# Two-layer transformer on one core: copies of the turned rows shared between ScalarE and VectorE, and four smaller moves in layer 1's attention

## The chip, the cores and the metric

The kernel runs on 1 core of one Trainium2 chip. The metric is the device time of the whole program in microseconds; the median of the timed runs is compared before and after. A core has a matrix engine (TensorE, PE), three engines for elementwise work (VectorE, DVE; ScalarE, ACT; GpSimd, POOL) and queues that start transfers (SyncE, SP, and GpSimd's own for gathers). Each engine works through its own instructions in order, and waits on semaphores for the others. TensorE writes to PSUM, which has eight banks here, each with room for 128 x 512 float32.

## The reference

Two layers, each attention and then a feed-forward part, with a layer norm (no scale) after each residual, on x of 8 x 512 x 512 float32. Layer 0 has causal attention with 16 heads and eight experts of which each token takes two. Layer 1, cut to what matters here:

```python
# attention: 8 heads of 64, keys and values shared by 4 heads each
nrm = norm(x, axis=-1) * d ** -0.5
h = norm_scale * x / (nrm + 1e-8) * split_scale
q, k, v = h @ Wq.T, h @ Wk.T, h @ Wv.T
attn = softmax(q @ k.T / sqrt(64))
x = layernorm(x + (x + (attn @ v) @ Wo.T))
# feed-forward, weights as integers: W = (wq - 128) * scale
x = layernorm(x + (silu(x @ Wg.T) * (x @ Wu.T)) @ Wd.T)
```

## The kernel before

The rows are worked in 8 batches of 512 tokens; a batch has NT = 4 tiles of 128 rows and ND = 4 slices of 128 columns. The stages follow each other: attention of layer 0, routing and expert tiles, attention of layer 1 (`Attention1.batches`, about 1189 to 1772 us of the profile), and the integer feed-forward (`IntegerFfn`). The change lies in layer 1's attention.

**Preparing a batch** (`Attention1.prepare`): its rows are the experts' results. `fetch` gathers two rows for each token (GpSimd starts the transfers, L673). They are weighted and added to x, tile by tile, either by `add` on VectorE (two L680, then `stat`: L694 and L695) or, in the first batch of the stage, partly by `sum` on GpSimd (two pairs L689, L690 for a tile) with `stat` in a later step. `deviations` (GpSimd, L701 to L703) and `norm` (VectorE, L710, L711, four L714) make the normalised rows xn. `turn(c)` transposes column slice c of the four tiles by TensorE into one bank of PSUM (L1477) and copies it, scaled, to hT (L1478, ScalarE). `key`, `value` and `query` multiply hT with the weights (L1484, L1493, L1503), and ScalarE copies the results out.

**The batch itself** is run in eight steps of two units each, a unit being a pair of heads g and a tile of keys kt. In each step, TensorE first makes the scores of its two units (`score`, L1579), which ScalarE exponentiates (L1582); VectorE adds the exponentials of the step before to a total (`add`, L1590: one instruction in odd steps, two in even ones); then the step's other work is issued from the list `todo`; then TensorE multiplies the exponentials of the step before with the values (`product`, L1601). After the fourth tile of keys, `normalise` sums the total over the partitions by TensorE (L1609, to a bank "rs"), copies it by ScalarE (L931), inverts it (VectorE, L1612), scales the head pair's output (L1613), and GpSimd adds the inverse to a guard's total (L934).

**The list of other work** (`plan`): step 0 issues the gathers of batch b + 1, and queries go to steps 0, 1 and 3 (1, 3 and 5 in the first batch, 0, 1 and 5 in the last). From the second batch on, steps 2 to 5 `project` batch b - 1, a tile each (L1551; `residual`: L1557 and the statistics L1561, L1562; after the fourth tile GpSimd's L1565 and L1566 make rstd), and step 6 first normalises batch b - 1 on VectorE (`norm`, four L1572, which need rstd), then turns the four slices of batch b + 1 and projects its keys; step 7 makes its values and first query. In the last batch, steps 4 and 6 turn and split batch 0's rows for the feed-forward instead (`split`: L1022 on TensorE, L1023 on ScalarE, L1024 on VectorE). `weights.convert` (L994, L926) turns integer weights to floats in steps 1 and 7.

**What sets the order.** While this stage runs, `in_order` fixes the order of TensorE, VectorE, ScalarE and GpSimd to the one in which the code issues. Before it, among the expert tiles, only TensorE is so fixed, and after it, in the feed-forward, a scheduler places the instructions. PSUM: two banks, "mm", are shared by all of `self.mm` (turned slices, projections, "rs"); four hold scores, two hold the heads' outputs. Exponentials have four buffers.

**The first batch** is prepared piece by piece between expert tiles (`first_pieces`); the second is prepared inside the first, and so on.

**The end of the stage**: after the last step the remaining sums are made, then the last batch is projected with all four tiles' banks open: three of four head groups for each tile, `norm` of batch 6, then the fourth group of each tile, followed by `residual`. The feed-forward starts with L1055 (gate and up, 16 instructions each), L1058 on ScalarE, L1060 on VectorE, the split of the hidden values (L1063, L1064) and the down product L1069, whose weights come from L994.

Of the kernel before, what the change touches and what calls it, by code (L numbers as in the profile page):

```python
# [13 lines left out]
AF = mybir.ActivationFunctionType  # L14
ALU = mybir.AluOpType
# [3 lines left out]
P = 128  # L19
NB = 8  # L20
S = 512
D = 512
NT = S // P
ND = D // P
# [48 lines left out]
class Env:  # L73
# [19 lines left out]
    def open_stream(self, ctx, batches, **kw):  # L93

        resident = ctx.enter_context(self.tc.tile_pool(name=f"resident{batches[0]}", bufs=1, **kw))
        for b in batches:
            self.xs[b] = resident.tile([P, NT, D], F32, tag=f"x{b}", name=f"x_{b}")
# [904 lines left out]
class IntegerFfn:  # L1002
# [9 lines left out]
    def split(self, b, c, ps):  # L1012


        nc = self.nc
        if c == 0:
            pool = self.work if b % 2 else self.rows
            self.halves[b] = [pool.tile([P, ND, S], F32R, tag=f"rows{i}", name=f"x3_{part}")
                              for i, part in enumerate(("high", "low"))]
        high, low = self.halves[b]  # L1020
        for t in range(NT):
            nc.tensor.transpose(ps[:, ts(t, P)], self.env.xs[b][:, t, ts(c, P)], self.env.ident)  # L1022
        nc.scalar.copy(high[:, c, :], ps)  # L1023
        nc.vector.tensor_tensor(low[:, c, :], ps, high[:, c, :].bitcast(F32), ALU.subtract)  # L1024
# [420 lines left out]
class Attention1:  # L1445
# [17 lines left out]
    def prepare(self, b):  # L1463


        nc, own, w_qkv = self.nc, self.own, self.w_qkv
        st = self.state[b] = {"qT": [None] * ND}
        combine = Combine(self.router, b, self.rows, ("rows0", "rows1"))

        def norm():  # L1470
            st["xn"], st["scale"] = combine.norm()
            st["hT"] = own.tile([P, ND, S], F32, tag="hT", name="hT1")

        def turn(c):
            ps = self.mm([P, S], "ps_hT")
            for t in range(NT):
                nc.tensor.transpose(ps[:, ts(t, P)], st["xn"][:, t, ts(c, P)], self.env.ident)  # L1477
            nc.scalar.activation(st["hT"][:, c, :], ps, AF.Copy, scale=self.nss[:, c : c + 1])  # L1478

        def key():  # L1480
            hT = st["hT"]
            ps = self.mm([P, S], "ps_k1")
            for c in range(ND):
                nc.tensor.matmul(ps, lhsT=w_qkv[:, 4, ts(c, P)], rhs=hT[:, c, :], start=c == 0, stop=c == ND - 1)  # L1484
            st["kT"] = own.tile([P, S], F32, tag="kT", name="kT", bufs=2)
            nc.scalar.copy(st["kT"], ps)

        def value():
            hT = st["hT"]
            ps = self.mm([P, NT, P], "ps_v1")  # L1490
            for t in range(NT):
                for c in range(ND):
                    nc.tensor.matmul(ps[:, t, :], lhsT=hT[:, c, ts(t, P)], rhs=w_qkv[:, 5, ts(c, P)],  # L1493
                                     start=c == 0, stop=c == ND - 1)
            st["v"] = own.tile([P, NT, P], F32, tag="v", name="v1", bufs=2)
            nc.scalar.copy(st["v"], ps)

        def query(g):

            hT = st["hT"]  # L1500
            ps = self.mm([P, S], "ps_q1")
            for c in range(ND):
                nc.tensor.matmul(ps, lhsT=w_qkv[:, c, ts(g, P)], rhs=hT[:, c, :], start=c == 0, stop=c == ND - 1)  # L1503
            st["qT"][g] = (self.work if g % 2 else own).tile([P, S], F32, tag="qT", name="qT")
            nc.scalar.copy(st["qT"][g], ps)  # L1505

        return {"fetch": combine.fetch, "add": combine.add, "sum": combine.sum, "stat": combine.stat, "deviations": combine.deviations, "norm": norm,
                "turn": turn, "key": key, "value": value, "query": query}

    def first_pieces(self):  # L1510
# [15 lines left out]
    def batches(self, work, p_sc, p_av, weights, split):  # L1526
        env, nc, guard, state, HD = self.env, self.nc, self.guard, self.state, self.HD
        xs = env.xs
        scale = 1.0 / math.sqrt(HD)
# [14 lines left out]
        def project(b, t):  # L1544
            ps = self.mm([P, D], "ps_o1")
            project_groups(b, t, ps, range(ND))
            residual(b, t, ps)

        def project_groups(b, t, ps, groups):
            for c in groups:  # L1550
                nc.tensor.matmul(ps, lhsT=state[b]["aoT"][:, c, ts(t, P)], rhs=w_out[:, c, :],  # L1551
                                 start=c == 0, stop=c == ND - 1)

        def residual(b, t, ps):
            st = state[b]
            x = xs[b][:, t, :]
            nc.vector.scalar_tensor_tensor(x, x, st["scale"][t], ps, ALU.mult, ALU.add)  # L1557
            if t == 0:
                st["stats"] = small.tile([P, NT, 6], F32, name="stats1")
                st["mv"] = small.tile([P, NT, 2], F32, name="mv1")  # L1560
            nc.vector.bn_stats(out=st["stats"][:, t, :], in_=x)  # L1561
            nc.vector.bn_aggr(out=st["mv"][:, t, :], in_=st["stats"][:, t, :])  # L1562
            if t == NT - 1:
                st["rstd"] = rstd = small.tile([P, NT], F32, name="rstd1")
                nc.gpsimd.tensor_scalar(rstd, st["mv"][:, :, 1], LN_EPS, None, ALU.add)  # L1565
                nc.gpsimd.tensor_tensor(rstd, rstd, env.neg_half, ALU.pow)  # L1566

        def norm(b):
            st = state.pop(b)
            for t in range(NT):  # L1570
                x = xs[b][:, t, :]
                nc.vector.tensor_scalar(x, x, st["mv"][:, t, 0:1], st["rstd"][:, t : t + 1], ALU.subtract, ALU.mult)  # L1572
# [43 lines left out]
        def plan(b):  # L1616


            todo = [[] for _ in range(ND * NT // 2)]
            here = pieces.pop(b)  # L1620
            first, final = b == 0, b == NB - 1
            then = None if final else self.prepare(b + 1)
            if not final:
                pieces[b + 1] = then
                todo[0] += [lambda t=t: then["fetch"](t) for t in range(NT)]
            for g, i in zip((1, 2, 3), (1, 3, 5) if first else (0, 1, 5) if final else (0, 1, 3)):
                todo[i].append(lambda g=g: here["query"](g))
            if b:
                for t, i in enumerate((2, 3, 4, 7) if final else (2, 3, 4, 5)):
                    todo[i].append(lambda t=t: project(b - 1, t))  # L1630
                if not final:
                    todo[6].append(lambda: norm(b - 1))
            if final:
                for c, i in enumerate((4, 6, 6, 6)):
                    todo[i].append(lambda c=c: split(0, c, self.mm([P, S], "ps_xT")))
            else:
                if first:

                    for t, i in ((1, 1), (2, 2), (3, 3)):
                        todo[i].append(lambda t=t: then["sum"](t))  # L1640
                        todo[i + 1].append(lambda t=t: then["stat"](t))
                for t, i in ((0, 2),) if first else ((0, 2), (1, 2), (2, 3), (3, 4)):
                    todo[i].append(lambda t=t: then["add"](t))
                todo[4].append(then["deviations"])

                todo[5].insert(0, then["norm"])
                todo[6] += [lambda c=c: then["turn"](c) for c in range(ND)]
                todo[6].append(then["key"])
                todo[7] += [then["value"], lambda: then["query"](0)]
            for i in (7,) if first else (1, 7):  # L1650
                todo[i] += [weights.convert, lambda: weights.load(work, 2, weights.FIRST)]
            return todo

        last = []
        for b in range(NB):
            for i, thunks in enumerate(plan(b)):
                units = [(b, u // NT, u % NT) for u in (2 * i, 2 * i + 1)]
                ps = [score(*unit) for unit in units]
# [4 lines left out]
                sums = [product(*unit) for unit in last]  # L1663
# [3 lines left out]
        for unit in last:  # L1667
            add(*unit)
        sums = [product(*unit) for unit in last]
        sums[-1]()  # L1670

        b = NB - 1
        banks = [self.mm([P, D], "ps_o1") for _ in range(2)]
        banks += [p_sc.tile([P, 2, S], F32, tag="sc", name="ps_o1")[:, 0, :] for _ in range(2)]
        for t in range(NT):
            project_groups(b, t, banks[t], range(ND - 1))
        norm(b - 1)
        for t in range(NT):
            project_groups(b, t, banks[t], (ND - 1,))
            residual(b, t, banks[t])  # L1680
        return lambda: norm(b)


# [346 lines left out]
```

## Time and profile before

| | us |
|---|---|
| timed runs (3): median | 2297.6 |
| timed runs: lowest and highest | 2297.3, 2299.71 |
| the profiled execution: its own time | 2295.71 |
| the profiled execution: span from first to last instruction | 2293.9 |
| one batch of layer 1's attention (from one L1484 to the next, 1308.40 to 1381.47) | 73.1 |
| mean granted TensorE clock over the span | 0.994 |

The span is what the profile's times count from; the execution's own time has 1.8 us more around it. A line of the timeline gives the start, the time and the engine, then the program's line and the names of what is written and read; in square brackets stands how long the engine was idle before it and which engine's instruction ended that. "xN" says that N instructions were merged. PE stands for matmuls, PEld for loads of weights, which overlap them. A float32 matmul of 512 columns appears as two records.

### The profile page before, as it was taken

What the parts mean: (1) busy time and instruction counts of PE and PEld (TensorE: products, weight loads), DVE (VectorE), ACT (ScalarE), POOL (GpSimd) and SP (SyncE); (2) the same over time, 40 slices, a digit from 0 to 9 for tenths busy, and PEclk for the clock granted to TensorE, in tenths of its full rate; (3) what the DMA queues carried; (4) which work ended last, traced back from release to release, by engine and by line L of the source; (5) the groups of instructions that cost most, each with busy time, mean ns of one, the idle gap of its engine ahead of it and who ended that gap; (6) DMA issues with size and microseconds to landing.
All of it is one profiled execution on the core that took longest, in us unless ns stands there. A gap on an engine that the chain in (4) does not pass through costs nothing.

```text
span 2293.9 us, 24187 instructions
## 1 busy us (share of the span) xinstructions
PE 2240.5 (98%) x9430; PEld 1154.8 (50%) x9430; DVE 1245.0 (54%) x1974; ACT 648.2 (28%) x937; POOL 501.6 (22%) x493
## 2 busy tenths in 40 slices
PE   9999999999999999999998999999998999999997
PEld 3344444444444444444443334443343878888876
DVE  3457575666668432242216877777667544444443
ACT  2332323323324221111223323333332322222222
POOL 2231323413224231131125122321211000000000
PEclk9999999999999999999999999999999999999999
DMA  8010110101112234332233011100100100000000
GB/s 289 19 56 1 55 33 23 56 7 49 54 38 84 92 115 146 93 120 91 87 127 94 10 55 56 55 29 17 37 1 23 42 19 19 19 19 19 19 19 20
DMA packets 58444, 126.63 MB, mean 55 GB/s; under 512 B 6210, under 2 KB 6210, under 8 KB 58322
## 3 DMA queue, kind: packets, MB, share of 16 engines
q1 hardware_dynamic: 47040, 89.32, 11.1%
q0 software_dynamic: 10560, 34.61, 5.2%
q8 instruction: 77, 1.26, 0.2%
q10 hardware_dynamic: 722, 1.07, 0.1%
q14 instruction: 45, 0.37, 0.1%
HBM read 89.59 MB, written 35.39 MB: 54 GB/s over the span
## 4 chain that ended last, share of the span: by engine, by line
PE 76%; issue 8%; DVE 7%; DMA 4%; POOL 4%; ACT 2%; POOLq 0%; SPq 0%; ACTq 0%; DVEq 0%
PE ps_f L1069 7%; PE ps_g L1055 6%; PE ps_u L1055 6%; PE ps_gu L845 5%; PE ps_o L1216 5%; PE ps_o L1551 5%; PE av L1601 5%; PE sc L1579 4%; PE ps_q L1503 4%; PE ps_q L1200 4%; PE ps_k L1208 4%; PE ps_v L1193 4%; PE av L1288 3%; PE sc L1264 3%; PE ps_y L862 2%
## 5 line engine op out<-in xcount | busy, mean ns | idle before, releaser
L845 PE MATMUL ps_gu<-experts,xrT 128*128 128x512 f32 (+1 forms) x520 | 248.6, 601 | 0.0
L1268 ACT ACTIVATE p<-sc 128x2048 f32<-128x2048 f32 (+1 forms) x96 | 152.9, 1593 | 189.0 <-PE sc L1264 182.1
L1273 POOL TENSOR_SCALAR_AFFINE_SELECT p<-p 128x512 f32<-128x512 f32 x128 | 92.1, 734 | 380.1 <-ACT p L1268 376.6
L1060 DVE SCALAR_TENSOR_TENSOR hT<-ps_u,vec,sg 128x512 f32<-128x512 f32 x88 | 65.8, 748 | 201.4 <-PE ps_u L1055 201.4
L1069 PE MATMUL ps_f<-ffn_w,h_half 128*128 128x512 f32 x672 | 169.4, 392 | 1.1 <-DVE h_half L1064 1.1
L934 POOL TENSOR_TENSOR g_total<-g_total,r_inv 128x512 f32<-128x512 f32 x64 | 89.7, 1402 | 361.4 <-DVE r_inv L1612 286.2
L1612 DVE RECIPROCAL r_inv<-r_inv 128x512 f32<-128x512 f32 x32 | 106.8, 3339 | 105.4 <-ACT r_inv L931 105.4
L1582 ACT ACTIVATE p<-sc 128x1024 f32<-128x1024 f32 x128 | 124.1, 1021 | 130.3 <-PE sc L1579 119.7
L1296 DVE TENSOR_TENSOR p<-p 128x1536 f32<-128x1536 f32 (+2 forms) x96 | 129.3, 1346 | 38.5 <-POOL p L1273 21.5
L1055 PE MATMUL ps_g<-x_high,ffn_w 128*128 128x512 f32 x352 | 141.5, 402 | 3.0 <-DVE x L1557 3.0
L1069 PEld LDWEIGHTS ps_f<-ffn_w,h_half 128*128 128x128 f32 x672 | 124.5, 188 | 33.7 <-DVE h_half L1064 7.2
L848 DVE TENSOR_TENSOR h<-ps_gu,h 128x256 f32<-128x256 f32 x67 | 28.4, 424 | 205.2 <-ACT h L847 205.2
L1055 PE MATMUL ps_g<-x_low,ffn_w 128*128 128x512 f32 x352 | 139.4, 396 | 0.0
L1055 PE MATMUL ps_u<-x_high,ffn_w 128*128 128x512 f32 x352 | 139.2, 395 | 0.0
L1055 PE MATMUL ps_u<-x_low,ffn_w 128*128 128x512 f32 x352 | 139.2, 395 | 0.0
L1579 PE MATMUL sc<-qT,kT 64*128 64x512 f32 x512 | 127.9, 618 | 1.0 <-ACT qT L1505 0.7
L862 PE MATMUL ps_y<-experts,hT 128*128 128x512 f32 (+1 forms) x272 | 127.9, 592 | 0.5 <-ACT hT L856 0.5
L1200 PE MATMUL ps_q<-experts 128*128 128x512 f32 x256 | 120.4, 611 | 4.4 <-DMA experts<-in_xT 4.4
L845 PEld LDWEIGHTS ps_gu<-experts,xrT 128*128 128x128 f32 x520 | 89.6, 192 | 68.0 <-issue 68.0
L1601 PE MATMUL av<-p,v 128*64 128x512 f32 x512 | 123.8, 605 | 0.0
L1193 PE MATMUL ps_v<-experts 128*128 128x512 f32 x256 | 116.3, 602 | 2.4 <-DVE v L1195 2.4
L1208 PE MATMUL ps_k<-experts 128*128 128x512 f32 x256 | 117.5, 602 | 0.2 <-ACT r_inv L931 0.2
(256 smaller groups left out, 3544.5 us busy)
## 6 DMA issues: line engine op xcount, KB each, us to landing
results<-y SPq DMA_DIRECT2D x68, 256.0 KB
x<-in_x SPq DMA_DIRECT2D x8, 1024.0 KB
experts<-in_gate_up SPq DMA_DIRECT2D x8, 1024.0 KB
rows<-x SPq DMA_DIRECT2D x32, 256.0 KB
x<-rows SPq DMA_DIRECT2D x8, 1024.0 KB
experts<-in_xT SPq DMA_DIRECT2D x7, 1024.0 KB
out<-x SPq DMA_DIRECT2D x28, 256.0 KB
ffn_i<-in_wq_ffn SPq DMA_DIRECT2D x11, 512.0 KB
```

What stands on the lines that cost most here:

```text
L845: mm = nc.tensor.matmul(ps, lhsT=xT[:, c, :], rhs=self.weights(i, c), start=c == 0, stop=c == ND - 1)
L862: self.nc.tensor.matmul(ps, lhsT=hT[:, c, :], rhs=self.weights(i, ND + c), start=c == 0, stop=c == self.NI - 1)
L1055: nc.tensor.matmul(ps, lhsT=w[:, ts(dc, P)], rhs=x[:, dc, :], start=(dc, i) == (0, 0), stop=(dc, i) == (ND - 1, 1))
L1069: self.nc.tensor.matmul(os[t], lhsT=h[:, ts(t, P)], rhs=self.weights(2 * NHID + c), start=(c, i) == (0, 0), stop=(c, i) == (NHID - 1, 1))
L1193: nc.tensor.matmul(ps, lhsT=xts[b][:, c, ts(t, P)], rhs=wv[:, c, :], start=c == 0, stop=c == ND - 1)
L1200: nc.tensor.matmul(ps, lhsT=wq[:, g, ts(c, P)], rhs=xts[b][:, c, :], start=c == 0, stop=c == ND - 1)
L1208: nc.tensor.matmul(ps, lhsT=wk[:, g, ts(c, P)], rhs=xts[b][:, c, :], start=c == 0, stop=c == ND - 1)
L1268: nc.scalar.activation(p, sc[:, :, :width], AF.Exp, scale=scale)
L1296: nc.vector.tensor_tensor(total[:, :, P * kt :], total[:, :, P * kt :], p[:, :, at : at + w], ALU.add)
L1579: nc.tensor.matmul(sc[:, j, :], lhsT=st["kT"][hs, ts(kt, P)], rhs=st["qT"][g][hs, :], start=True, stop=True)
L1582: nc.scalar.activation(p, sc, AF.Exp, scale=scale)
L1601: nc.tensor.matmul(st["av"][HD * j : HD * (j + 1), :], lhsT=st["v"][:, kt, HD * j : HD * (j + 1)], rhs=p[:, j, :], start=kt == 0, stop=kt ...
```

## The change

Five edits, all in layer 1's attention.

1. `turn`: of the four copies of a batch's turned slices, those of c = 1 and 3 are made by VectorE (`tensor_scalar`), those of c = 0 and 2 stay with ScalarE. This holds for all eight batches, the first (among the expert tiles) too.
2. First batch: tiles 0 and 1 of the next batch are added on VectorE in steps 1 and 2, tiles 2 and 3 on GpSimd from steps 1 and 2, with their statistics two steps later. Before, tile 0 was added on VectorE in step 2, and tiles 1 to 3 on GpSimd from steps 1 to 3, with statistics one step later.
3. Last batch: the four splits of batch 0 go to steps 0, 2, 4 and 6, one each, instead of one in step 4 and three in step 6.
4. `residual` is cut into `residual` (L1557) and `statistics`. `project` still calls one after the other; at the end of the stage the four residuals come first and the four tiles' statistics after them.
5. At the end of the stage, the first bank is taken and the first three groups of tile 0 are issued ahead of the last sums (`sums[-1]()`); the second "mm" bank is taken after them.

```diff
-            nc.scalar.activation(st["hT"][:, c, :], ps, AF.Copy, scale=self.nss[:, c : c + 1])
+            if c % 2:
+                nc.vector.tensor_scalar(st["hT"][:, c, :], ps, self.nss[:, c : c + 1], None, ALU.mult)
+            else:
+                nc.scalar.activation(st["hT"][:, c, :], ps, AF.Copy, scale=self.nss[:, c : c + 1])
...
             residual(b, t, ps)
+            statistics(b, t)
...
             nc.vector.scalar_tensor_tensor(x, x, st["scale"][t], ps, ALU.mult, ALU.add)
+
+        def statistics(b, t):
+            st = state[b]
+            x = xs[b][:, t, :]
             if t == 0:
                 st["stats"] = small.tile([P, NT, 6], F32, name="stats1")
...
             if final:
-                for c, i in enumerate((4, 6, 6, 6)):
+                for c, i in enumerate((0, 2, 4, 6)):
                     todo[i].append(lambda c=c: split(0, c, self.mm([P, S], "ps_xT")))
             else:
                 if first:
 
-                    for t, i in ((1, 1), (2, 2), (3, 3)):
+                    for t, i in ((2, 1), (3, 2)):
                         todo[i].append(lambda t=t: then["sum"](t))
-                        todo[i + 1].append(lambda t=t: then["stat"](t))
-                for t, i in ((0, 2),) if first else ((0, 2), (1, 2), (2, 3), (3, 4)):
+                        todo[i + 2].append(lambda t=t: then["stat"](t))
+                for t, i in ((0, 1), (1, 2)) if first else ((0, 2), (1, 2), (2, 3), (3, 4)):
                     todo[i].append(lambda t=t: then["add"](t))
...
         sums = [product(*unit) for unit in last]
+
+        b = NB - 1
+        banks = [self.mm([P, D], "ps_o1")]
+        project_groups(b, 0, banks[0], range(ND - 1))
         sums[-1]()
-
-        b = NB - 1
-        banks = [self.mm([P, D], "ps_o1") for _ in range(2)]
+        banks.append(self.mm([P, D], "ps_o1"))
         banks += [p_sc.tile([P, 2, S], F32, tag="sc", name="ps_o1")[:, 0, :] for _ in range(2)]
-        for t in range(NT):
+        for t in range(1, NT):
             project_groups(b, t, banks[t], range(ND - 1))
         norm(b - 1)
         for t in range(NT):
             project_groups(b, t, banks[t], (ND - 1,))
             residual(b, t, banks[t])
+        for t in range(NT):
+            statistics(b, t)
         return lambda: norm(b)
```

## The prediction

> **What bounds the kernel now.** I read the busy times first, then the chain of waits, TensorE's waits in the changed stage (1188 to 1800 us), and the timeline around each.
>
> ```profile
> PE 2240.5 (98%) x9430; PEld 1154.8 (50%) x9430; DVE 1245.0 (54%) x1974; ACT 648.2 (28%) x937; POOL 501.6 (22%) x493
> ...
> PE 76%; issue 8%; DVE 7%; DMA 4%; POOL 4%; ACT 2%; POOLq 0%; SPq 0%; ACTq 0%; DVEq 0%
> ```
>
> TensorE (PE) is busy 98% of the span and leads the chain: an edit gains what it takes out of TensorE's gaps and loses what it adds to them. TensorE's waits in the stage:
>
> ```profile
> PE rs L1609 <- DVE total L1590: 6.5, 2, 4.9
> PE ps_hT L1477 <- ACT hT L1478: 3.6, 7, 0.8
> PE ps_g L1055 <- DVE x L1557: 3.0, 1, 3.0
> PE ps_xT L1022 <- DVE x_low L1024: 1.4, 1, 1.4
> PE ps_k L1484 <- ACT hT L1478: 1.4, 7, 0.2
> ```
>
> Columns: total us, times, longest. The change aims at these 15.9 us. Its largest edit, to the turnings, aims at 5.0 us in seven places; this is the second of them, in batch 1:
>
> ```profile
> 1305.09 1.40 PE L1477 MATMUL ps_hT<-ident,xn 128*128 128x128 f32 x8
> ...
> 1306.22 1.27 ACT L1478 ACTIVATE hT<-ps_hT,nss 128x512 f32<-128x512 f32 x2
> ...
> 1306.64 2.52 DVE L1590 TENSOR_TENSOR total<-total,p 128x1024 f32<-128x1024 f32 x2
> 1306.81 1.11 POOL L1565 TENSOR_SCALAR rstd<-mv 128x4 f32<-128x4 f32 x1 [5.03 <-DVE mv L1562]
> ...
> 1306.96 1.23 PE L1477 MATMUL ps_hT<-ident,xn 128*128 128x128 f32 x8 [0.47 <-ACT hT L1478]
> ...
> 1307.66 1.27 ACT L1478 ACTIVATE hT<-ps_hT,nss 128x512 f32<-128x512 f32 x2 [0.17 <-PE ps_hT L1477]
> 1308.00 2.05 POOL L1566 TENSOR_TENSOR rstd<-rstd,neg_half 128x4 f32<-128x4 f32 x1
> 1308.40 0.30 PEld L1484 LDWEIGHTS ps_k<-hT,attn_qkv 128*128 128x128 f32 x2 [0.44 <-ACT hT L1478]
> ...
> 1310.09 1.91 DVE L1572 TENSOR_SCALAR x<-x,mv,rstd 128x512 f32<-128x512 f32 x4 [0.93 <-POOL rstd L1566]
> ```
>
> Columns: start, duration, engine, line, instruction, idle time before it. Here ScalarE (ACT) is free and copies at once; VectorE (DVE) is working off L1590 and then waits for GpSimd's (POOL) L1566 before L1572.
>
> **Turnings, batches 1 to 6.** The copies of c = 1 and 3 go to VectorE, whose order in this stage is fixed by the program: the changed program issues them behind L1590 x2 and L1572 x4 (batch b-1's normalisation), none of which the change moves. That an instruction of VectorE doesn't overtake a waiting one, the first batch shows: L694 waited 9.26 us for GpSimd until 1205.88, and L680 behind it began only at 1206.70, though its rows had landed long before (they are the first two gathers, and GpSimd's L689 used the third at 1199.99). So the copy of c = 1 starts when L1572 ends, 1310.09 + 1.91 = 1312.00. No row has this copy on VectorE: nearest are L162, a plain copy from PSUM (681 ns), and L1202, a scaled one (750 ns). I take 0.75: done at 1312.75. From copy to TensorE the row shows 0.10 (c = 0's copy ends 1306.86, turning at 1306.96).
>
> In the changed program's waits the third and fourth turnings wait for ScalarE's copies alone; the key projection L1484 waits for VectorE's copy of c = 1. So TensorE turns c = 2 at 1306.96 as now, ScalarE copies it by about 1308.25, c = 3 is turned by 1308.9, and L1484 starts at 1312.85 instead of 1308.40: 4.45 us later, after 3.95 us of idle. The copy of c = 3 (to 1313.5) hides behind the first three quarters of L1484 (until 1312.85 + 3 x 0.86 = 1315.4); without that cover it would cost 0.75. Behind the two copies on VectorE stands L1612, whose sums TensorE delivers later still: nobody else waits. The other five batches show the same rows (0.47, 0.93 and 0.20 at 1380.0, 1383.2, 1381.5, and at 1672.4, 1675.5, 1673.8): 6 x 4.45 = 26.7 us. The saved wait of 0.67 is already taken off. If VectorE's work before the copy took the 0.68 copy or met no GpSimd contention in the normalisation, 0.1 each.
>
> **The clock behind these gaps.** Two gaps of TensorE in this stage are of that size, 4.87 and 3.00 us. Stretches of 5 us (busy times of PE, PEld, DVE, ACT, POOL; the granted clock; DMA):
>
> ```profile
> 1215.00:1220.00 5.00, 0.22 (x2) 0.00 (x0) 4.86 (x5) 1.94 (x2) 4.92 (x3) 1.00 0.00 0
> 1220.00:1225.00 5.00, 4.91 (x13) 1.63 (x14) 2.15 (x4) 1.84 (x4) 3.80 (x5) 0.66 0.01 3
> ...
> 1775.00:1780.00 5.00, 4.75 (x14) 3.75 (x15) 3.46 (x7) 1.72 (x2) 1.27 (x2) 0.66 0.51 197
> ```
>
> After each the clock is 0.66 over 5 us. L1609 to the next L1503 takes 4.50 us there (1220.09 to 1224.59) against 2.88 (1202.99 to 1205.87): 1.6 us. The 1.67 us gap before 1757.24 shows no such thing. A gap of 3.95 lies between the two that did; its place against the throttle's phase is unknown, so per gap 0 to 1.6. I take five of six: 8.0 us (bounds 0 and 9.6).
>
> [...]
>
> **Turnings elsewhere.** In batch 0 no L1572 stands in front: L1590 ends at 1234.15, the copy of c = 1 at 1234.9, the fourth turning (there it needs that bank) starts 0.45 later than 1234.46 and, without the present wait of 0.20, L1484 at 1235.5 instead of 1235.32: +0.2. Among the expert tiles two copies of 0.69 leave ScalarE for VectorE, which idles 3.82 us before its next L848: nothing; without that cover 2 x 0.75.
>
> **First batch's sums.** GpSimd loses two of six L689/L690 pairs, VectorE gets two L680 more (0.75 each) and stands no longer idle 9.26 us in L694:
>
> ```profile
> 1205.88 0.69 DVE L694 BATCH_NORM_STATS2 stats<-x 128x6 f32<-128x512 f32 x1 [9.26 <-POOL x L690]
> ...
> 1220.09 1.97 PE L1609 MATMUL rs<-total,ones 128*64 128x512 f32 x4 [4.87 <-DVE total L1590]
> ```
>
> The first two L680 now stand before the L1590 pair that the sums at 1202.99 need. Of those gathers, 83 packets of the gather queue's 640 had moved by 1197 and 240 by 1199, so, at 80 for each gather, the two land about 1197.4 and 1198.5, and at latest 1199.99. L680 ends 1199.25, L694/L695 0.87 later, L1590 x2 (2.56 alone, 3.4 beside GpSimd, the row at 1216.64) at about 1203.5: a wait of 0.5 (0 to 2). Then L680 x2 to 1205.6, statistics 1206.5, L1612/L1613 1210.5, L1590 1212.2, L694/L695 of t = 2 (GpSimd has its sum by about 1208) 1213.1, L1590 x2 1216.2, while the next sums are due at 1215.7: 0.5 (0 to 1). So 4.87 + 1.6 of clock - 1.0 = 5.5 us saved (3 to 6.5).
>
> **Last batch's splits.** One for each of four steps; L1024 (0.69) hides behind L1601 (1.94): the wait of 1.41 goes. -1.4 (0 to -1.4).
>
> **Last sums first.** Three L1551 groups of t = 0 (2.57) cover the 1.67 us wait of L1609. What is late next: banks[1] now takes the bank of rs and waits for ScalarE's L931, which starts 1.17 after L1609 and takes 0.60, against 1.01 when L1551 followed at once: +0.8. TensorE ends L1551 at 1771.1 instead of 1772.25. The fourth L1557, with the statistics moved behind, ends about 1.0 after its group, so L1055 starts at 1772.15 instead of 1775.25, after a gap of 1.05 that leaves the clock alone (1.6): 4.7 us by the end of the first two hidden groups, 1779.7. There TensorE meets VectorE: statistics to 1775.5, L1572 x2 to 1778.1, L994 (1.22) 1779.3, L1060 1780.05, L926 (2.28) 1782.3, L1064 1783.0 for L1069's low halves. TensorE stands some 1.5 us. -3.1 (-1.1, where nothing but the sums' wait is saved, to -4.7).
>
> **Sum**, against the profiled execution of 2295.7 (span 2293.9 and 1.8 around it): 26.7 + 8.0 + 0.2 - 5.5 - 1.4 - 3.1 = +24.9, so 2320.6. The median of the timed runs lies 1.9 above that execution: 2297.6 + 24.9 = 2322.5; I say 2322.
>
> **Rivals.**
> - The copies meet a free VectorE and the alternation does what it looks like. Then 3.6 + 1.4 = 5.0 us go besides 5.5, 1.4 and 3.1: 2297.6 - 15.0 = 2282.6, faster. It decides at L1572: the copy would have to start before about 1307.7, 4.3 us ahead of L1572's end. For it: VectorE is busy only 54%. Against it: the three timelines read, 300 us apart, show the same queue. 5%.
> - The gaps don't throttle the clock. For it: 3.95 is below the 4.87 that did so at once. 2322.5 - 8.0 = 2314.5. 20%.
> - The gathers are late and the end gives nothing: L680 holds the sums back for the full 2 us, the splits and VectorE's chain before L1069 eat the rest. First batch -3, splits 0, end -1.1, six throttled gaps: 26.7 + 9.6 + 0.2 - 4.1 = 32.4, so 2330. For it: all queues are full from 1191 to 1213. Against it: L689 found its rows at 1199.99. 13%.
>
> **Numbers.** The forecast itself 62%. Range 2312 (no throttling, and 2.5 better at the end or with the gathers) to 2331 (the late case); only the first rival and the rims lie outside. About 0.2% (4.6 us) is what a measurement can tell from no change: faster 0.05, same 0.02, slower 0.93.
>
> **What would show it.** In batches 1 to 6 the key projection waits some 4 us for VectorE's hT, and the granted clock falls behind it; a batch takes some 79 us instead of 73.1. L1609's wait near 1220 falls below 1 us, L1022's is gone, L1055's falls to about 1. Wrong if the copies of c = 1 start within a us of their turning, or if the fourth turning waits as well.

## The result, and the profile after

| | before | changed |
|---|---|---|
| timed runs measured together (4 each): median, us | 2297.45 | 2325.67 |
| lowest to highest, us | 2291.89 to 2299.71 | 2323.04 to 2326.34 |
| profiled execution: own time, span, us | 2295.71, 2293.9 | 2326.34, 2324.6 |
| mean granted TensorE clock | 0.994 | 0.987 |

The changed kernel is slower: the ratio is 1.0124, with a 95% interval of 1.0105 to 1.0144. Forecast were 2322 us, in a range from 2312 to 2331.

Below, the lines of the attention of layer 1 have shifted: turnings L1477 as before; ScalarE's copy is L1481 and VectorE's L1479; keys L1487 (were L1484); scores L1587 (L1579); sums of exponentials L1598 (L1590); partition sums L1617 (L1609); rstd L1573, L1574 (L1565, L1566); normalisation L1580 (L1572); residual L1561 (L1557); projection L1555 (L1551).

First the busy times and the chain's shares of the changed kernel's page:

```profile
PE 2253.9 (97%) x9430; PEld 1158.6 (50%) x9430; DVE 1257.3 (54%) x1992; ACT 638.3 (27%) x921; POOL 494.8 (21%) x489
...
PE 20%; DVE 2%; POOL 1%; issue 0%; ACT 0%; POOLq 0%
```

TensorE has the same 9430 instructions and is busy for 13.4 us more (2253.9 against 2240.5): the same work took longer, which is the clock. The span grew by 30.7, so the other 17.3, on balance, are idle time. The chain is of no use this time: its shares add up to 23%, so followed back from the end (the feed-forward) it stops short of the turnings. So I went to TensorE's waits from 1188 to 1840 us (total, times, longest):

```profile
PE ps_k L1487 <- DVE hT L1479: 22.1, 6, 3.7
PE ps_hT L1477 <- ACT hT L1481: 8.0, 13, 0.8
PE ps_hT L1477 <- DVE hT L1479: 1.1, 1, 1.1
PE ps_g L1055 <- DVE x L1561: 0.8, 1, 0.8
PE ps_o L1555 <- ACT r_inv L931: 0.8, 1, 0.8
...
PE rs L1617 <- DVE total L1598: 0.2, 1, 0.2
```

The waits that the smaller edits aimed at are gone or small: the sums' 6.5 us are 0.2, L1022's 1.4 stands nowhere, L1055's 3.0 are 0.8. In their place stands a new one, six times 3.7 us: the keys wait for VectorE's copy. The timeline of batch 1 shows why (start, duration, engine, line, instruction, idle time before it):

```profile
1301.46 1.41 PE L1477 MATMUL ps_hT<-ident,xn 128*128 128x128 f32 x8
...
1303.02 2.52 DVE L1598 TENSOR_TENSOR total<-total,p 128x1024 f32<-128x1024 f32 x2
1303.19 1.11 POOL L1573 TENSOR_SCALAR rstd<-mv 128x4 f32<-128x4 f32 x1 [5.04 <-DVE mv L1570]
1303.33 0.66 PE L1477 MATMUL ps_hT<-ident,xn 128*128 128x128 f32 x4 [0.46 <-ACT hT L1481]
...
1304.38 2.06 POOL L1574 TENSOR_TENSOR rstd<-rstd,neg_half 128x4 f32<-128x4 f32 x1
1304.77 0.66 PE L1477 MATMUL ps_hT<-ident,xn 128*128 128x128 f32 x4 [0.78 <-ACT hT L1481]
1306.47 1.91 DVE L1580 TENSOR_SCALAR x<-x,mv,rstd 128x512 f32<-128x512 f32 x4 [0.93 <-POOL rstd L1574]
1308.30 1.40 DVE L1479 TENSOR_SCALAR hT<-ps_hT,nss 128x512 f32<-128x512 f32 x2
1309.10 5.36 PE L1487 MATMUL ps_k<-hT,attn_qkv 128*128 128x512 f32 x8 [3.67 <-DVE hT L1479]
```

The bank of c = 1 was turned by about 1302.9, but VectorE works through its queue first: the two sums, 0.93 us of waiting for GpSimd's rstd, the four normalisations. Its copies begin at 1308.30, 5.4 us after the turning. The keys start 7.64 us after the first turning, where it was 3.31 before: 4.33 later. And then they take 5.36 us instead of 3.70. That second loss is the clock's. Here are stretches of 3.41 us of the changed kernel, laid so that they end where the granted clock changes, in batches 1, 2 and 3 (busy time of PE, PEld, DVE, ACT, POOL with their instructions; granted clock; DMA):

```profile
1302.24:1305.65 3.41, 1.94 (x12) 1.23 (x12) 3.16 (x4) 1.73 (x3) 2.38 (x2) 1.00 0.00 0
1305.65:1309.06 3.41, 0.00 (x0) 0.00 (x0) 2.59 (x6) 0.00 (x0) 0.78 (x1) 1.00 0.00 0
1309.06:1312.47 3.41, 3.37 (x4) 1.52 (x5) 0.64 (x1) 0.00 (x0) 0.00 (x0) 0.50 0.00 0
1312.47:1315.88 3.41, 3.41 (x13) 1.20 (x13) 0.00 (x0) 0.58 (x1) 0.00 (x0) 1.00 0.00 0
...
1384.14:1387.56 3.42, 0.35 (x4) 0.11 (x2) 2.49 (x6) 0.00 (x0) 1.36 (x1) 1.00 0.00 0
1387.56:1390.97 3.41, 2.80 (x4) 1.25 (x5) 1.22 (x2) 0.00 (x0) 0.00 (x0) 0.50 0.00 0
1390.97:1394.38 3.41, 3.41 (x6) 1.27 (x4) 0.00 (x0) 0.00 (x0) 0.00 (x0) 0.50 0.00 0
1394.38:1397.80 3.42, 3.42 (x16) 0.97 (x16) 0.00 (x0) 0.61 (x2) 0.00 (x0) 1.00 0.00 0
...
1462.65:1466.06 3.41, 1.31 (x8) 0.83 (x8) 2.38 (x4) 0.87 (x2) 3.16 (x2) 1.00 0.00 0
1466.06:1469.47 3.41, 0.82 (x1) 0.50 (x2) 3.19 (x6) 0.00 (x0) 0.00 (x0) 0.50 0.00 0
1469.47:1472.89 3.42, 3.42 (x5) 1.33 (x4) 0.00 (x0) 0.00 (x0) 0.00 (x0) 0.50 0.00 0
1472.89:1476.30 3.41, 3.41 (x14) 1.15 (x14) 0.00 (x0) 0.58 (x1) 0.00 (x0) 1.00 0.00 0
```

In these rows the clock is 1.00 or 0.50 for a whole window. The windows lie on one grid: from the end of the slow stretch at 1312.47 to the one at 1394.38 there are 24 windows of 3.413 us. In these rows, a window in which TensorE was busy for 0.00, 0.35 or 1.31 us is followed by one at half clock; a half-clock window that is busy almost throughout (3.37) is the last, and one that is not (2.80, 0.82) is followed by another. So here the price of a gap is half of TensorE's busy time in the slow windows, and it depends on where on the grid the gap falls: (1312.47 - 1309.10) / 2 = 1.7 in batch 1, (1394.38 - 1388.17) / 2 = 3.1 in batch 2, (1472.89 - 1468.65) / 2 = 2.1 in batch 3. All six, from the keys' rows:

| batch | 1 | 2 | 3 | 4 | 5 | 6 | sum |
|---|---|---|---|---|---|---|---|
| keys L1487, start, us | 1309.10 | 1388.17 | 1468.65 | 1548.15 | 1627.16 | 1707.63 | |
| duration, us | 5.36 | 6.77 | 5.79 | 5.30 | 6.75 | 5.77 | |
| above 3.70 of before, us | 1.66 | 3.07 | 2.09 | 1.60 | 3.05 | 2.07 | 13.5 |

The pattern comes back after three batches, which is what a fixed grid would do: 1548.15 - 1309.10 = 239.05 us are 70.04 windows.

The place where the sums waited before, in the changed kernel:

```profile
1215.00:1220.00 5.00, 5.00 (x24) 1.46 (x20) 2.70 (x4) 2.50 (x5) 4.83 (x6) 1.00 0.10 22
1220.00:1225.00 5.00, 5.00 (x16) 1.92 (x16) 4.83 (x3) 2.44 (x4) 2.74 (x2) 1.00 0.00 0
```

TensorE is busy throughout and the clock stays at 1.00. Before, TensorE worked for 0.22 us in the first of these two stretches, and the clock over the second was 0.66.

### The profile page after: what moved, and what is told of

Read it like the earlier page. It is cut to its first block, busy times and chain, and to the rows that moved or that the text cites. A ratio compares the mean times of both kernels' runs of the same rounds, so it can differ in the third digit from the quotient of the medians.

```text
span 2324.6 us, 24176 instructions
## 1 busy us (share of the span) xinstructions
PE 2253.9 (97%) x9430; PEld 1158.6 (50%) x9430; DVE 1257.3 (54%) x1992; ACT 638.3 (27%) x921; POOL 494.8 (21%) x489
## 5 line engine op out<-in xcount | busy, mean ns | idle before, releaser
L1590 ACT ACTIVATE p<-sc 128x1024 f32<-128x1024 f32 x128 | 124.0, 1021 | 126.5 <-PE sc L1587 124.1
L1055 PE MATMUL ps_g<-x_high,ffn_w 128*128 128x512 f32 x352 | 141.2, 401 | 0.8 <-DVE x L1561 0.8
L1055 PE MATMUL ps_g<-x_low,ffn_w 128*128 128x512 f32 x352 | 138.9, 395 | 0.0
L1055 PE MATMUL ps_u<-x_high,ffn_w 128*128 128x512 f32 x352 | 138.7, 394 | 0.0
L1055 PE MATMUL ps_u<-x_low,ffn_w 128*128 128x512 f32 x352 | 138.7, 394 | 0.0
L1587 PE MATMUL sc<-qT,kT 64*128 64x512 f32 x512 | 127.2, 615 | 1.0 <-ACT qT L1508 0.7
L1609 PE MATMUL av<-p,v 128*64 128x512 f32 x512 | 123.8, 605 | 0.0
L1555 PE MATMUL ps_o<-attn_out,aoT 128*128 128x512 f32 x256 | 117.3, 602 | 0.8 <-ACT r_inv L931 0.8
```

Of the source, the lines that this page charges most:

```text
L1055: nc.tensor.matmul(ps, lhsT=w[:, ts(dc, P)], rhs=x[:, dc, :], start=(dc, i) == (0, 0), stop=(dc, i) == (ND - 1, 1))
L1587: nc.tensor.matmul(sc[:, j, :], lhsT=st["kT"][hs, ts(kt, P)], rhs=st["qT"][g][hs, :], start=True, stop=True)
L1590: nc.scalar.activation(p, sc, AF.Exp, scale=scale)
L1609: nc.tensor.matmul(st["av"][HD * j : HD * (j + 1), :], lhsT=st["v"][:, kt, HD * j : HD * (j + 1)], rhs=p[:, j, :], start=kt == 0, stop=kt ...
```

## The experiments

The first four kernels ran on one chip, beside a median of 2297.56 us of the kernel before (14 runs, 2292.95 to 2300.5); the other four on another, beside 2298.95 (15 runs, 2293.33 to 2302.04). Single runs of one kernel differ by 4 to 13 us, so effects of a few us are read from the traces, between fixed points of the program.

**1. Four edits without the copies.** The changed kernel, with all copies on ScalarE again.

```diff
-            if c % 2:
-                nc.vector.tensor_scalar(st["hT"][:, c, :], ps, self.nss[:, c : c + 1], None, ALU.mult)
-            else:
-                nc.scalar.activation(st["hT"][:, c, :], ps, AF.Copy, scale=self.nss[:, c : c + 1])
+            nc.scalar.activation(st["hT"][:, c, :], ps, AF.Copy, scale=self.nss[:, c : c + 1])
```

> The changed kernel with all four copies of the turned rows back on ScalarE; the other four edits stay. Theory (VectorE's queue makes the copy late, and the throttled clock follows): six waits of 4.33 us (26.0) and their six slow clocks (13.5, read as what L1487 takes over 3.70 us in the profile of the changed kernel) go, and about 0.8 in batch 0: 2325.7 - 40.3 = about 2285, some 12 below the kernel before; a batch takes 73.1 us again. Rival (the loss comes from another of the edits, the new order of the first sums or of the end): it stays near 2325.

Measured: 2284.25 us (2278.77 to 2286.63, 5 runs), ratio 0.9937 [0.9916, 0.9957], clock 0.994. A batch takes 73.08 us again and the keys 3.70. So one edit costs 41.4 us (2325.67 - 2284.25) and the other four bring 13.3 (2297.56 - 2284.25). This version is faster than both kernels.

**2. The copies alone**, on the kernel before: the same lines added.

> The kernel before with the first edit alone: the copies of c = 1 and 3 on VectorE. Theory: 26.0 us of waits and 13.5 of clock on top of 2297.5, so about 2337; L1609's wait of 4.9 us near 1220, L1022's 1.4 and L1055's 3.0 stay as they were. Rival (the edits only cost together): near 2297.

Measured: 2334.03 us (2333.49 to 2337.34, 4 runs), ratio 1.0168 [1.0147, 1.019]. TensorE's waits in its trace:

```profile
PE ps_k L1487 <- DVE hT L1479: 22.0, 6, 3.7
...
PE rs L1612 <- DVE total L1593: 6.5, 2, 4.9
PE ps_g L1055 <- DVE x L1560: 3.0, 1, 3.0
PE ps_xT L1022 <- DVE x_low L1024: 1.4, 1, 1.4
```

The new wait is there in full with none of the other edits, and the old waits stand beside it. The six slow keys come back too, 5.30, 6.76, 5.78, 5.29, 6.75 and 5.78 us, within 0.06 us of the changed kernel's row for row; why both kernels meet the grid in the same way is not shown. By the medians the copies cost 36.5 us here (39.5 were expected) and 41.4 in experiment 1; the profiled span is 37.9 us longer than that of the kernel before, although the stage begins 1.5 us earlier (first scores at 1188.00). The loss belongs to the copies; the other edits neither make nor mend it.

**3. The normalisation behind the turnings.** Is it VectorE's queue, or a copy that is slow in itself? In step 6 of the changed kernel, `norm(b - 1)` is issued after the keys.

```diff
-                if not final:
-                    todo[6].append(lambda: norm(b - 1))
...
                 todo[6].append(then["key"])
+                if b:
+                    todo[6].append(lambda: norm(b - 1))
```

> The changed kernel with step 6's normalisation of batch b-1 (four L1580) issued after the turnings and the keys, so that on VectorE only the two sums L1598 stand before the copies. Theory (it is VectorE's queue): the copy of c = 1 starts when L1598 ends, so from the first turning to the keys 5.5 us instead of 7.6: 12.8 us less in six batches. The gap of TensorE falls from 3.7 to some 2.4 us; whether one of that length still throttles the clock no run shows yet: 2299 if not, 2312 if as before. Rival (the copy is slow on VectorE wherever it stands, or its hand-over to TensorE is): no change, 2325.

Measured: 2300.48 us (2294.79 to 2307.37, 10 runs), ratio 1.0015 [1.0003, 1.0028], clock 0.990; 25 us below the changed kernel. Its waits:

```profile
PE ps_hT L1477 <- DVE hT L1479: 14.7, 7, 2.3
PE ps_hT L1477 <- ACT hT L1481: 3.4, 7, 0.6
```

What is left is the wait behind the two sums of exponentials, 2.3 us, now at the fourth turning. The queue it is. The clock goes both ways here: the keys take 6.17 us in batch 1, 3.60 in batches 3 to 5 of one and the same profile. The windows of the grid in which that 2.26 us gap lies, in batch 1 and in batch 3:

```profile
1303.37:1306.78 3.41, 1.33 (x9) 0.84 (x8) 3.24 (x6) 1.88 (x3) 2.23 (x2) 1.00 0.00 0
1306.78:1310.19 3.41, 2.66 (x7) 1.63 (x8) 2.20 (x5) 0.00 (x0) 0.93 (x1) 0.50 0.00 0
1310.19:1313.61 3.42, 3.42 (x6) 1.35 (x5) 1.07 (x3) 0.00 (x0) 0.00 (x0) 0.50 0.00 0
...
1460.38:1463.79 3.41, 1.80 (x8) 1.08 (x9) 2.66 (x4) 0.07 (x1) 1.79 (x1) 1.00 0.00 0
1463.79:1467.20 3.41, 3.41 (x12) 1.23 (x12) 1.47 (x4) 0.59 (x1) 0.00 (x0) 1.00 0.00 0
```

The window with 1.33 us of work was followed by half clock, the one with 1.80 was not; in batch 6 one with 1.77 (1682.25 to 1685.66) was again. The same gap, put otherwise on the grid, cost (2.66 + 3.42) / 2 = 3.0 us or nothing. The length of the gap does not decide it here: in batch 0 a gap of 1.09 us was followed by half clock (keys 5.29 us), where in the changed kernel one of 1.11 was not (3.60). The median lies near the 2299 expected without the throttle, the profiled execution, 2306.62, half-way to the 2312 with it: the truth is some of each.

**4. The gap filled.** To part the wait from the clock, the fourth turning of batches 2 to 7 is written eight times, so that TensorE works while it waits; the results are the same.

```diff
-            for t in range(NT):
+            for t in [t for _ in range(8 if c == ND - 1 and b > 1 else 1) for t in range(NT)]:
                 nc.tensor.transpose(ps[:, ts(t, P)], st["xn"][:, t, ts(c, P)], self.env.ident)
```

> The changed kernel in which the fourth turning of batches 2 to 7 is written eight times over, the same result each time: 28 more transposes, some 3 us, fill TensorE's gap before the keys. Theory (the gap costs twice, by its wait and by the clock after it): L1487 starts as late as before, but at full clock, so 13.5 us less: about 2312, and L1487 takes 3.7 us in each batch. Rival (the slow keys have another cause, such as VectorE's copies reading the same banks): L1487 stays at 5.3 to 6.8 us and the time at 2325 or above.

Measured: 2309.72 us (2308.73 to 2313.31, 4 runs), ratio 1.0061 [1.0039, 1.0083], clock 0.995. Batch 1 in its trace:

```profile
1302.21 3.71 PE L1477 MATMUL ps_hT<-ident,xn 128*128 128x128 f32 x32 [0.78 <-ACT hT L1481]
1306.54 3.70 PE L1487 MATMUL ps_k<-hT,attn_qkv 128*128 128x512 f32 x8 [0.62 <-DVE hT L1479]
```

A batch takes 77.40 us, 4.32 above 73.08, and the keys 3.70 in each of batches 1 to 6. The keys start as late as in the changed kernel, 7.64 us after the first turning (1298.90), and what went is the clock's part: 2325.67 - 2309.72 = 16 us by the medians, 13.5 by the rows of the keys. The rest, in the profiles, lies ahead of the stage (first scores at 1189.49 against 1191.39) and in batch 0. The waits' part is 2309.72 - 2284.25 = 25.5, in the trace 6 x 4.32 = 25.9.

**5. Alternation with VectorE free.** In step 6 both the sums of exponentials and the normalisation go behind the keys.

```diff
-                if not final:
-                    todo[6].append(lambda: norm(b - 1))
...
-                for unit in last:
-                    add(*unit)
+                late = i == 6 and b < NB - 1
+                if not late:
+                    for unit in last:
+                        add(*unit)
                 for thunk in thunks:
                     thunk()
+                if late:
+                    for unit in last:
+                        add(*unit)
+                    if b:
+                        norm(b - 1)
```

> The changed kernel, but in step 6 of batches 0 to 6 VectorE's two sums of exponentials and the normalisation of batch b-1 are issued behind the turnings and the keys, so that VectorE stands free for the copy of c = 1 and can take it as soon as it is turned. My theory (the lateness came from VectorE's queue alone): no wait of several us is left, a batch takes 73.1 us, the keys 3.7 us. Whether the alternation is then worth anything is open between two readings. A: as in the prediction's first rival, the waits of 0.47 and 0.20 us before the third turning and the keys go, 7 x 0.67 = 4.7 us below the kernel in which ScalarE makes all copies (2284.3): about 2279.5. B: those waits are the time of single copies (c = 0's for the third turning's bank, c = 2's for the keys' bank), which two engines do not shorten: about 2284, and TensorE waits at L1477 and at the keys as there, some 3.4 and 1.4 us in all. I hold B the likelier. If the sums come too late for L1617's partition sums or the normalisation for anything else, a new wait stands in the page.

Measured: 2286.35 us (2280.77 to 2287.9, 4 runs), ratio 0.9938 [0.992, 0.9955]. The loss is gone whole. Batch 2 in its trace:

```profile
1373.05 1.94 ACT L1590 ACTIVATE p<-sc 128x1024 f32<-128x1024 f32 x2 [5.53 <-PE sc L1587]
...
1373.74 1.41 PE L1477 MATMUL ps_hT<-ident,xn 128*128 128x128 f32 x8
...
1374.87 0.69 ACT L1481 ACTIVATE hT<-ps_hT,nss 128x512 f32<-128x512 f32 x1
...
1375.30 0.72 DVE L1479 TENSOR_SCALAR hT<-ps_hT,nss 128x512 f32<-128x512 f32 x1
...
1375.62 1.12 PE L1477 MATMUL ps_hT<-ident,xn 128*128 128x128 f32 x8 [0.47 <-ACT hT L1481]
...
1376.31 0.69 ACT L1481 ACTIVATE hT<-ps_hT,nss 128x512 f32<-128x512 f32 x1 [0.75 <-PE ps_hT L1477]
1376.77 0.75 DVE L1479 TENSOR_SCALAR hT<-ps_hT,nss 128x512 f32<-128x512 f32 x1 [0.75 <-PE ps_hT L1477]
1377.05 3.70 PE L1487 MATMUL ps_k<-hT,attn_qkv 128*128 128x512 f32 x8 [0.32 <-ACT hT L1481]
```

VectorE now copies c = 1 within 0.2 us of its turning, and still nothing is won: from the first turning to the keys there are 3.31 us, as in experiment 1 (1371.99 to 1375.30) and before. The third turning waits for the bank that c = 0's copy frees (1374.87 + 0.69 = 1375.56), the keys for that of c = 2's (1377.00). Both copies are ScalarE's: that of c = 0 starts when the exponentials (L1590) are through, that of c = 2 as soon as its bank is turned. Neither waits for another copy, so a second engine for c = 1 and 3 shortens neither. Reading B holds.

**6, 7, 8. The small edits, each alone** on the kernel before. 6 is edit 2, 7 is edits 4 and 5, 8 is edit 3; in this order:

```diff
-                    for t, i in ((1, 1), (2, 2), (3, 3)):
+                    for t, i in ((2, 1), (3, 2)):
                         todo[i].append(lambda t=t: then["sum"](t))
-                        todo[i + 1].append(lambda t=t: then["stat"](t))
-                for t, i in ((0, 2),) if first else ((0, 2), (1, 2), (2, 3), (3, 4)):
+                        todo[i + 2].append(lambda t=t: then["stat"](t))
+                for t, i in ((0, 1), (1, 2)) if first else ((0, 2), (1, 2), (2, 3), (3, 4)):
```

```diff
+        banks = [self.mm([P, D], "ps_o1")]
+        project_groups(b, 0, banks[0], range(ND - 1))
         sums[-1]()
+        banks.append(self.mm([P, D], "ps_o1"))
...
+        for t in range(NT):
+            statistics(b, t)
```

```diff
-                for c, i in enumerate((4, 6, 6, 6)):
+                for c, i in enumerate((0, 2, 4, 6)):
```

> The kernel before with edit 2 alone (first batch's sums: tiles 0 and 1 on VectorE, 2 and 3 on GpSimd, statistics two steps later). Forecast of the prediction: -5.5 us (3 to 6.5), so about 2292; TensorE's wait of 4.87 us near 1220 falls below 1 us and the clock stays at 1.00 behind it, and from the first scores to the keys of batch 0 the time falls from 45.8 to about 40 us. If the gathers' rows came late (rival), L680 would hold L1590 and the sums back by up to 2 us: -3, so 2294.5.

> The kernel before with edits 4 and 5 alone (at the end of the stage the first three groups ahead of the last sums, the residuals ahead of the statistics). Forecast of the prediction: -3.1 us (1.1 to 4.7), so about 2294.5; in the changed kernel's trace the two pieces of it were -3.0 and -0.8. L1055's wait of 3.0 us falls to about 1, the sums' wait of 1.67 us goes, a wait of 0.8 us for L931 comes. If the end gives nothing beyond the sums' wait (rival), -1.1: 2296.5.

> The kernel before with edit 3 alone (last batch's splits in steps 0, 2, 4 and 6, one each). Forecast of the prediction: L1022's wait of 1.41 us goes and nothing else moves: -1.4, so about 2296, which the timed runs can hardly tell from no change; the trace can: from the keys of batch 6 to the first L1055, 101.46 us become about 100.05. If a wait of the same size comes elsewhere (VectorE's L1024 in the other steps), the stretch stays at 101.5.

Measured: 6: 2288.69 us (4 runs), ratio 0.9948 [0.9931, 0.9964]. 7: 2293.26 (6 runs), 0.9964 [0.9952, 0.9977]. 8: 2295.67 (10 runs), 0.9986 [0.9976, 0.9996]. These medians lie 10.3, 5.7 and 3.3 us below the kernel before, together 19.2 where experiment 1, which has all three, was 13.3 below: too rough for such effects. Between fixed points of the traces, in us:

| | before | changed | exp. 1 | exp. 6 | exp. 7 | exp. 8 |
|---|---|---|---|---|---|---|
| first scores of the stage start at | 1189.50 | 1191.39 | 1189.43 | 1192.36 | 1190.73 | 1192.15 |
| from there to batch 0's keys | 45.82 | 40.40 | 39.72 | 39.15 | 47.26 | 47.13 |
| keys of batch 6 to the first L1055 | 101.46 | 99.11 | 97.04 | 101.47 | 98.67 | 99.83 |
| L1055 to the end of the span | 518.65 | 517.86 | 517.84 | 518.36 | 517.88 | 518.43 |

The second row is the first batch: 6.1 (experiment 1) to 6.7 us saved (experiment 6). The third: the end alone saves 2.79, the splits alone 1.63, together 4.42, which is just what experiment 1 saves; the changed kernel's 99.11 has the slow keys of batch 6 in it (99.11 - 2.07 = 97.04). The fourth: the end saves another 0.8. The first row has nothing of the stage in it, and wanders by 2.9 us over these six profiles: at least that much a single profile is uncertain by.

Experiments 7 and 8 keep the old wait of the first batch's sums, and there the second row is 1.4 and 1.3 us longer than before. The windows of experiment 7 at that place:

```profile
1220.00:1225.00 5.00, 3.69 (x8) 1.14 (x10) 2.16 (x4) 0.69 (x2) 3.94 (x3) 0.58 0.01 3
1225.00:1230.00 5.00, 5.00 (x13) 1.85 (x10) 4.90 (x3) 2.05 (x2) 3.37 (x4) 0.74 0.00 0
```

The same wait (4.85 us here, 4.87 before) is followed by two windows at half clock, 1220.82 to 1227.64, where in the profile of before there was one, 1220.0 to 1223.4. One and the same gap costs 1.6 or 3.1 us, by the luck of the execution.

## Why the prediction was right, and where it was off

The terms of its sum, against the profiled executions:

| term | forecast | measured | read from |
|---|---|---|---|
| turnings, batches 1 to 6 | +26.7 | +26.0 | 6 x 4.33, batch 1's rows; experiment 4's period |
| the clock behind these gaps | +8.0 (0 to 9.6) | +13.5 | the six rows of L1487 |
| turning of batch 0 | +0.2 | +0.7 | 40.40 - 39.72, experiment 1 |
| first batch's sums | -5.5 (-3 to -6.5) | -6.1 | 39.72 - 45.82 |
| last batch's splits | -1.4 | -1.6 | experiment 8 |
| last sums first, and the end | -3.1 (-1.1 to -4.7) | -3.6 | experiment 7: 2.79 + 0.8 |
| ahead of the stage | 0 | +1.9 | first scores: 1191.39 - 1189.50 |
| sum | +24.9 | +30.8 | spans: 2324.6 - 2293.9 = +30.7 |

- **Ahead of the stage.** The 1.9 us are not the change's: the first turning, which stands before the first copy that was moved, is already late by them (1112.62 against 1110.72). From there to the first scores it is 78.8 us in both kernels, so the copies among the expert tiles cost nothing, as forecast.
- **The turnings** went as foretold: the queue of VectorE, the order of waits, the 0.75 us of the copy (0.70 in the trace) and 4.45 us for each batch (4.33). Experiments 2, 3 and 5 show the queue as the cause: without the normalisation in front the wait falls from 3.7 to 2.3, without the sums as well the keys follow the first turning as soon as before.
- **The clock is the term that was mis-sized.** The step that failed: "A gap of 3.95 lies between the two that did; its place against the throttle's phase is unknown, so per gap 0 to 1.6." The 1.6 was taken as the most that a gap can cost, and it was the price of one gap in one execution, one that met a single slow window. The place on the grid was known to be unknown, but was let decide only whether a gap is throttled, not for how long. Measured are 1.6 to 3.1, 2.26 on average, and no gap of the six was spared. In the sum the miss of 5.5 us is partly offset by somewhat larger gains elsewhere, and the timed medians moved by 28.2 rather than by the profile's 30.7.
- **The first batch**: both waits put in its place (0.5 each) were too cautious; 0.2 and none came. L680 began at 1199.86, which is 1197.97 when the 1.89 us are taken off by which the stage began later; 1197.4 was forecast.
- **Turning of batch 0**: the fourth turning waited 1.1 us for VectorE's bank, not 0.45. The prediction kept VectorE's two sums where they were, 0.40 us ahead of the first turning (1231.61 against 1232.01); now they start 0.37 behind it (1228.03 against 1227.66), and the copy after them is later by nearly as much.
- **The end**: the forecast wait of 0.8 for L931 came (0.84); L1055's gap was 0.84 instead of 1.05 and left the clock alone.
- **The rivals.** That the copies meet a free VectorE fell with the timeline, and its price was wrong as well: experiment 5 gave VectorE free and won none of the 5.0 us. That the gaps don't throttle fell with the windows; experiment 4 is the kernel it describes, 2309.7 against the 2314.5 worked out. That the gathers are late and the end gives nothing fell with experiments 6 and 7. The time of this third rival (2330) was hardly further off than the forecast's, for a reason that did not hold: the gains it left out stood in for a clock that it had too low as well.

## What to carry to other kernels

Work that is moved to an engine with idle time joins that engine's queue (here VectorE, 54% busy, began the copies 5.4 us after the turning): look at what is issued ahead of it, and what that waits for, at the moment when it is due, not at the share of busy time. Before a second engine is put on a chain of copies, see whether the wait is for a queue of copies or for the one copy that frees the bank; here it was the latter, and nothing could be won (experiment 5: 3.31 us from the first turning to the keys, as before). The gaps of TensorE in the changed kernel were paid twice, by their wait of 3.7 us and by the clock behind it, 1.6 to 3.1 us; those of 2.26 us in batches 3 to 5 of experiment 3 by their wait alone. The price read from one row is one draw, and a bound taken from it alone was too low, 1.6 against 3.1.

## What the runs showed of the hardware

- In the traces of the two kernels the granted clock is 1.00 or 0.50, and its changes lie on a grid of 3.413 us: in the kernel before there are 163 steps from 1219.99 to 1776.36, in the changed kernel 118 from 1309.06 to 1711.83. From the first scores of layer 1's attention to the first products of the feed-forward their slow stretches were one or two windows long, and so were the ones read in experiments 3 (1306.78 to 1313.61, two), 6 (1771.04 to 1774.45, one) and 7 (1220.82 to 1227.64, two).
- In that part of these traces, the windows at full clock with 0.00 to 1.33 us of TensorE work were followed by half clock, and those with 1.80 or more were not. In between it went both ways: 1.72 (1228.27 to 1231.69) and 1.77 in experiment 3 were followed by half clock, 1.74 in experiments 6 (1750.56 to 1753.97) and 8 (1757.87 to 1761.28) was not. So the busy time of the trace does not tell these apart. Among the expert tiles it does not tell at all: the changed kernel's TensorE is shown busy for all 3.41 us of 735.62 to 739.03, and half clock followed. What decides is not shown.
- A gap of 2.26 us cost 3.0 us of clock or nothing within one execution (experiment 3, batches 1 and 3), one of 4.87 us cost 1.6 us in the kernel before and the same one, 4.85 us, 3.1 in experiment 7: 1.5 us between two executions of the same code.
